# Moving two groups of buffers by 32 bytes within a partition: the split gated products of a mixture-of-experts kernel

## The chip, the cores and the metric

The kernel runs on one core of one Trainium2 chip. The metric is the device time of one execution in microseconds (us). The time before is the median of 3 runs, 1145.75 us (1145.21 to 1145.89).

## The reference, cut to what matters

The input is 16 sequences of 512 tokens with 128 features. Each goes through two residual steps:

```
x = x + layernorm(y),  y = C h + D * n,  h = causal convolution of B n,  n = layernorm(x)
x = x + layernorm(sum over 8 experts e of cw[e] * ( (silu(n G[e]) * (n U[e])) W[e] )),  n = layernorm(x)
```

The weights cw come from two softmaxes over the 8 experts. G, U and W are 128x512, 128x512 and 512x128 for each expert. This second step is nearly all of the work: for each of the 16 sequences ("blocks" b), each of the 8 experts e and each of the four quarters fc of the 512 hidden features, one tile of 128 hidden features x 512 tokens is computed and multiplied back down. That makes 16 x 8 x 4 = 512 tiles, numbered n.

## The kernel before, in words

**Splitting.** Products on TensorE use a 4-byte format (fp32r) that doesn't hold all of an fp32 number's digits. So each operand is split into two: a high part (`hi`, the number cast to fp32r) and a low part (`lo`, the number minus its high part). A product is then three matmuls, written in `mm3` (lines 336 to 339): weight-high by data-high (L337), weight-low by data-high (L338), weight-high by data-low (L339). The weight is the stationary operand of 128x128, which a separate instruction loads; the data are the moving operand of 128x512, which is streamed past it.

**One tile.** `up(n)` makes two such groups, g (gate) and uu (up), from the normalized and split input `xh`, `xl` of the block. ScalarE (ACT) takes the SiLU of g (L563). `gate` multiplies by uu on VectorE (DVE, L574); the result is called uu when it stays where it was, hh when it is put into SBUF. `split_hi` casts it on ACT into a buffer `hi` (L579), and `split_lo` subtracts on DVE or on GpSimd (POOL) into a buffer `lo` (L585). Four tiles later (LAG), `down(n)` streams that `hi` and `lo` past the third weight and accumulates the output d. Every four tiles `combine` multiplies d by the expert's weight and adds it up (L600, L605, L608). So TensorE's steady sequence is nine matmuls of 512 columns per tile: g three times, uu three times, d three times, with moving operands xh xh xl, xh xh xl, hi hi lo.

**Other work.** The front of the next blocks (layernorm, the convolution by a scan, the routing) and the back of the last ones are generators, cut into steps that the loop over n places by costs noted for DVE, ACT and POOL (`steps`, `take`, SLOT = 1.94 us). They add short groups to TensorE: bu (three matmuls of the same size, with moving operands `uh`, `ul`), yp and lg (small ones).

**Where buffers lie.** Memory on chip (SBUF) is addressed in bytes within each of 128 partitions. The pools are laid out in the order in which they are opened: const (weights, tables), fe (the blocks' inputs and intermediates: xh, xl, uh, ul and more), small (coefficients of a few bytes), and h, called `hp` in the code. hp holds `hi` and `lo` (5 buffers each of 2048 bytes), and sg, hh and ct (2 each). The total of the pools ahead decides at which byte hi and lo begin. In the built program every weight part and xh, xl, uh and ul begin 64 bytes past a multiple of 1024. All ten buffers hi and lo, and sg, hh and ct, begin 992 past one. The steps within a weight (the four quarters fc) are 512 bytes.

The first weights are loaded into buffers of hi and lo before these have other use, and two buffers of lo (`spare`) serve the first block.

Of the kernel before, what the change touches and what calls it, by code (L numbers as in the profile page):

```python
# [11 lines left out]
F32 = mybir.dt.float32  # L12
# [7 lines left out]
P = 128  # L20
# [27 lines left out]
def sandwich(ctx, tc, x, a_params, B_w, C_w, Dv, w_router, w_gating, w_gate, w_up, w_down, sines, out):  # L48
# [6 lines left out]
    small = pool("small", 3)  # L55
# [24 lines left out]
            nc.sync.dma_start(out=xts[b][:, k], in_=x[b].rearrange("(c p) d -> p c d", p=P)[:, k])  # L80


    spare = [hp.tile([P, F], F32R, name=f"spare{i}", tag="lo", bufs=LAG + 1).bitcast(F32) for i in range(2)]


# [785 lines left out]
```

## Time and profile before

| | |
|---|---|
| median of 3 runs | 1145.75 us |
| time of the profiled execution | 1146.53 us |
| its span, first to last instruction | 1144.7 us |
| granted TensorE clock, mean over the span | 0.997 |
| busy: PE, weight loads, DVE, ACT, POOL | 1121.9, 913.7, 870.9, 710.3, 764.9 us |
| HBM traffic | 61 GB/s |

PE is TensorE's matmuls and PEld its weight loads, which overlap them. A matmul's recorded length is not its share of the time: the next one starts while the last columns of the one before still pass through. The pace is the distance from one start to the next, and the timeline shows it.

### The profile page before, as it was taken

Reading aid. Unit: us, or ns where it says so; the run is one execution under the profiler, and the core shown is the slowest. Engines: PE = TensorE matmul, PEld = TensorE weight load, DVE = VectorE, ACT = ScalarE, POOL = GpSimd, SP = SyncE. Lnnn points to the kernel's source line nnn. Section 1 sums busy time; section 2 is a strip of 40 time slices with the busy share of each in tenths; the row PEclk is TensorE's granted clock in tenths of the full one; section 3 lists DMA queues with packets and bytes.
Section 4 is the critical chain, followed back from the end, with each engine's and each line's share of the span. In section 5 each row is a group of like instructions: output and inputs, shape, how many; then the busy total and the mean of one; then the engine's idle time right before and its main releaser. Section 6 shows DMA issues by size and latency. Waiting matters only on the chain.

```text
span 1144.7 us, 16089 instructions
## 1 busy us (share of the span) xinstructions
PE 1121.9 (98%) x4969; PEld 913.7 (80%) x4969; DVE 870.9 (76%) x2000; ACT 710.3 (62%) x1346; POOL 764.9 (67%) x641
## 2 busy tenths in 40 slices
PE   7999999999999999999999999999999999999997
PEld 4678787888888888888888888888888888888885
DVE  7878777787878778787777878777777877867666
ACT  3775655665666665666666665666666565666563
POOL 1788685775858668595866858677685776748452
PEclk9999999999999999999999999999999999999999
DMA  4140302203131120312202130121302202021120
GB/s 154 65 139 1 121 28 79 70 11 111 37 93 47 53 87 19 111 37 67 74 29 93 35 114 28 54 70 45 102 29 74 74 19 74 29 74 29 32 71 10
DMA packets 65894, 71.23 MB, mean 62 GB/s; under 512 B 8624, under 2 KB 50320, under 8 KB 65808
## 3 DMA queue, kind: packets, MB, share of 16 engines
q1 hardware_dynamic: 65392, 70.04, 19.8%
q8 instruction: 39, 0.64, 0.2%
q14 instruction: 47, 0.39, 0.1%
q10 hardware_dynamic: 416, 0.16, 0.1%
HBM read 54.98 MB, written 15.20 MB: 61 GB/s over the span
## 4 chain that ended last, share of the span: by engine, by line
PE 82%; DVE 2%; DMA 1%; issue 0%; ACT 0%; SPq 0%; DVEq 0%
PE d L337 9%; PE g L337 9%; PE d L338 9%; PE d L339 9%; PE g L338 9%; PE uu L337 9%; PE uu L339 9%; PE g L339 9%; PE uu L338 9%; PE yp L386 1%; PE lg L414 1%; DVE uu L574 1%; DMA cwb<-scw 0%; DVE lo L585 0%; ACT hi L579 0%
## 5 line engine op out<-in xcount | busy, mean ns | idle before, releaser
L579 ACT CAST hi<-uu 128x512 fp32r<-128x512 f32 x334 | 195.9, 587 | 219.7 <-DVE uu L574 200.4
L585 POOL TENSOR_TENSOR lo<-hh,hi 128x512 fp32r<-128x512 f32 x178 | 233.5, 1312 | 147.4 <-ACT hi L579 144.6
L563 ACT ACTIVATE sg<-g 128x512 f32<-128x512 f32 x512 | 306.7, 599 | 22.5 <-PE g L339 16.7
L585 DVE TENSOR_TENSOR lo<-uu,hi 128x512 fp32r<-128x512 f32 x334 | 229.1, 686 | 113.0 <-ACT hi L579 107.0
L574 DVE TENSOR_TENSOR uu<-sg,uu 128x512 f32<-128x512 f32 x334 | 231.2, 692 | 108.6 <-ACT sg L563 102.0
L608 POOL TENSOR_TENSOR acc<-acc,ct 128x512 f32<-128x512 f32 x109 | 145.3, 1333 | 119.2 <-DVE ct L605 107.1
L579 ACT CAST hi<-hh 128x512 fp32r<-128x512 f32 x178 | 110.6, 621 | 163.9 <-DVE hh L574 161.6
L337 PE MATMUL g<-xh,wgh 128*128 128x512 f32 x512 | 205.8, 402 | 2.3 <-ACT sg L563 1.5
L337 PE MATMUL uu<-xh,wuh 128*128 128x512 f32 x512 | 200.3, 391 | 5.7 <-DVE lo L585 5.7
L337 PE MATMUL d<-hi,wdh 128*128 128x512 f32 x512 | 203.5, 397 | 0.0
L338 PE MATMUL d<-hi,wdl 128*128 128x512 f32 x512 | 201.9, 394 | 0.0
L338 PE MATMUL g<-xh,wgl 128*128 128x512 f32 x512 | 201.3, 393 | 0.0
L339 PE MATMUL d<-lo,wdh 128*128 128x512 f32 x512 | 201.0, 393 | 0.0
L339 PE MATMUL g<-xl,wgh 128*128 128x512 f32 x512 | 199.8, 390 | 0.0
L339 PE MATMUL uu<-xl,wuh 128*128 128x512 f32 x512 | 199.6, 390 | 0.0
L338 PE MATMUL uu<-xh,wul 128*128 128x512 f32 x512 | 199.5, 390 | 0.0
L432 POOL TENSOR_TENSOR ez<-bases,ez 128x8 f32<-128x8 f32 x120 | 195.0, 1641 | 0.0
L574 DVE TENSOR_TENSOR hh<-sg,uu 128x512 f32<-128x512 f32 x178 | 120.9, 679 | 14.4 <-ACT sg L563 8.5
L337 PEld LDWEIGHTS uu<-xh,wuh 128*128 128x128 f32 x512 | 96.2, 188 | 29.9 <-DVE lo L585 7.9
L337 PEld LDWEIGHTS g<-xh,wgh 128*128 128x128 f32 x512 | 96.3, 188 | 25.8 <-ACT sg L563 4.6
L339 PEld LDWEIGHTS d<-lo,wdh 128*128 128x128 f32 x512 | 96.9, 189 | 23.4
L339 PEld LDWEIGHTS g<-xl,wgh 128*128 128x128 f32 x512 | 96.4, 188 | 23.2 <-DVE xl L754 0.4
(173 smaller groups left out, 1330.0 us busy)
## 6 DMA issues: line engine op xcount, KB each, us to landing
cwb<-scw SPq DMA_DIRECT2D x64, 512.0 KB
xt<-in_L_attn_u_dram SPq DMA_DIRECT2D x15, 256.0 KB
sco<-ob SPq DMA_DIRECT2D x60, 64.0 KB
ot<-sco SPq DMA_DIRECT2D x15, 256.0 KB
out_dram<-x SPq DMA_DIRECT2D x15, 256.0 KB
scr_u<-blk_u SPq DMA_DIRECT2D x52, 64.0 KB
ft_u<-scr_u SPq DMA_DIRECT2D x13, 256.0 KB
scr_x<-blk_x SPq DMA_DIRECT2D x52, 64.0 KB
```

The source lines that it names most:

```text
L337: pe.matmul(ps, w[0][:, cs], mh, start=first, stop=False)
L338: pe.matmul(ps, w[1][:, cs], mh, start=False, stop=False)
L339: pe.matmul(ps, w[0][:, cs], ml, start=False, stop=last)
L386: pe.matmul(yp[:, c], v[:, P * c : P * c + P], cT, start=True, stop=True)
L414: pe.matmul(lg[:, 2 * c : 2 * c + 2], xT[:, P * c : P * c + P], wrg.rearrange("d g e -> d (g e)"), start=True, stop=True,)
L432: gp.tensor_tensor(ez[:, i], bases.rearrange("p c g e -> p (c g) e")[:, i], ez[:, i], ALU.pow)
L563: act.activation(s, g, AF.Silu)
L574: vec.tensor_tensor(h, s, u, ALU.mult)
L579: act.copy(hi, pend[n])
L585: (gp if lo_pool[n] else vec).tensor_tensor(lo, h, hi.bitcast(F32), ALU.subtract)
L608: add = lambda: eng.tensor_tensor(acc, acc, t, ALU.add)
```

## The change

One tile of 8 fp32 numbers (32 bytes of each partition) is allocated in the pool small. Nothing writes or reads it.

```
@@ -80,6 +80,7 @@
             nc.sync.dma_start(out=xts[b][:, k], in_=x[b].rearrange("(c p) d -> p c d", p=P)[:, k])
 
 
+    small.tile([P, 8], F32, name="fill", bufs=1)
     spare = [hp.tile([P, F], F32R, name=f"spare{i}", tag="lo", bufs=LAG + 1).bitcast(F32) for i in range(2)]
```

In the built program the instructions of every engine are the same, in the same order, with the same operands and waits. The start addresses of the tiles of small and of hp are 32 bytes higher; those of const and fe, of PSUM and of DRAM stay. So hi, lo, sg, hh and ct begin at a multiple of 1024 bytes in place of 992 past one. Line numbers from 83 on rise by one.

More of the change, by code (lines that the diff above doesn't have):

```diff
@@ L80, in load_x @@
             nc.sync.dma_start(out=xts[b][:, k], in_=x[b].rearrange("(c p) d -> p c d", p=P)[:, k])
+    small.tile([P, 8], F32, name="fill", bufs=1)
     spare = [hp.tile([P, F], F32R, name=f"spare{i}", tag="lo", bufs=LAG + 1).bitcast(F32) for i in range(2)]
```

## The prediction

> **What bounds the kernel now.** First I read the page: busy shares and slices.
>
> ```profile
> PE 1121.9 (98%) x4969; PEld 913.7 (80%) x4969; DVE 870.9 (76%) x2000; ACT 710.3 (62%) x1346; POOL 764.9 (67%) x641
> ...
> PE   7999999999999999999999999999999999999997
> ```
>
> PE is busy 98% of the span. A high share alone could hide short waits, so next I asked for busy time by stretches, and for PE's waits in the long middle one.
>
> ```profile
> 75.00:200.00 125.00, 121.47 (x544) 98.82 (x543) 95.17 (x217) 77.70 (x150) 91.69 (x77) 1.00 0.20 65
> 200.00:1125.00 925.00, 925.00 (x4131) 760.79 (x4131) 704.54 (x1536) 581.50 (x1093) 630.41 (x515) 1.00 0.19 59
> ```
>
> The columns are the length, then busy time of PE, PEld, DVE, ACT, POOL, then clock and DMA. From 200 to 1125 us PE is busy 925.00 of 925.00, the clock is full, and the list of PE's waits in that stretch is empty. In these 925 us nothing but PE's own pace counts: matmuls times the distance from start to start.
>
> So third, that pace by kind: PE's groups in a clean stretch of 40 us.
>
> ```profile
> L339 PE MATMUL g<-xl,wgh 128*128 128x512 f32 x20 | 7.8, 389 | 0.0
> L337 PE MATMUL uu<-xh,wuh 128*128 128x512 f32 x20 | 7.8, 389 | 0.0
> ...
> L337 PE MATMUL d<-hi,wdh 128*128 128x512 f32 x19 | 7.6, 397 | 0.0
> L337 PE MATMUL g<-xh,wgh 128*128 128x512 f32 x19 | 7.5, 395 | 0.0
> L338 PE MATMUL d<-hi,wdl 128*128 128x512 f32 x19 | 7.5, 394 | 0.0
> L339 PE MATMUL d<-lo,wdh 128*128 128x512 f32 x19 | 7.4, 392 | 0.0
> ```
>
> The number before the last bar is the mean recorded length. Four of the nine kinds are at 389 ns (two uu rows are left out here); g's second, also left out, is at 393. The three d are at 397, 394, 392, and the two g that follow d at 395 and 393. Size, clock and weight loads (188 ns each) are the same. The nine lengths sum to 3527 ns; nine times 389 is 3501. The tile pays 26 ns over the fast kind.
>
> A recorded length is not a pace, so fourth the timeline, where no d stands among the matmuls and where nothing but d does.
>
> ```profile
> 274.54 0.39 PE L337 MATMUL g<-xh,wgh 128*128 128x512 f32 x1
> ...
> 275.90 0.40 PE L337 MATMUL d<-hi,wdh 128*128 128x512 f32 x1
> ...
> 1133.73 0.39 PE L337 MATMUL d<-hi,wdh 128*128 128x512 f32 x1
> ...
> 1136.31 0.40 PE L339 MATMUL d<-lo,wdh 128*128 128x512 f32 x1
> ```
>
> From 274.54 to 275.90 lie six matmuls of g and uu that follow a bu group and not d: 1.36 / 6 = 226.7 ns each. From 1133.73 to 1136.31 lie eleven of d alone at the end: 2.58 / 11 = 234.5 ns. And a whole tile in the steady part takes (271.78 - 230.45) / 20 = 2.0665 us between starts of the same kind. Six at 226.7 leave 706 ns for three d, 235.5 each. So a group that streams hi and lo costs 23 (by the tail) to 26 ns (by the tile) more than one that streams xh and xl. The two slow g after d are aftermath of d: where bu follows d, its first two are slow in the same way (273.85 to 274.31), and the g after bu are not.
>
> **Why the buffers may be the reason.** What differs between d and the other kinds? The weights of all begin 64 past a multiple of 1024, their quarters step by 512 bytes, and the four quarters have the same pace. The PSUM bank isn't it: behind d, bu writes yet another bank and shows the steps of g. The slot of hi and lo (five of each) doesn't show. What is left is where the moving operand begins: xh, xl, uh, ul at 64 past 1024, hi and lo at 992. The first is a multiple of 64, the second 32 off one. After the change hi and lo are multiples of 64 as well.
>
> **The change part by part.**
>
> *Instructions:* none added, removed or moved. No queue (SP's and POOL's included) holds anything new, and no wait is added.
>
> *Streaming hi and lo on PE.* No row shows a start at a multiple of 1024. The nearest are xh, xl and uh, ul, 226.7 ns. I take that: the gain per tile is 2066.5 - 9 x 226.7 = 26 ns. From 200 to 1125 us there are 432 tiles: 11.3 us. Before 200 us about 35 tiles run at the regular pace where PE carries the chain: 0.9 us. From 165 to 197 us the chain of waits runs along DVE (uu L574, lo L585, ct), and a DMA of 4.08 us (cwb<-scw); what PE saves there, 16 x 0.026 = 0.4 us, it waits away, and I count none. After 1125 us four tiles and the last d groups: 0.2 us. Sum 12.4 us.
>
> *The other engines' accesses to the moved tiles* (hi, lo, sg, hh, ct, and small). Compare the same operation on tiles that stay: ACT's cast of hh is 621 ns, of ft_x and ft_u 612 and 616; POOL's subtraction 1312 against 1292; DVE's product hh 679, the product v<-bu,tre 686. So between 9 ns less and 7 more each on ACT and DVE, and 20 less on POOL. This is worth nothing to the end: per tile DVE has 704.54 / 432 = 1.63 us of work, POOL 1.46, ACT 1.35, beside 2.07 for PE. That work covers it, also at 2.04. Were the cover gone, three operations of 7 ns on a tile would be 21 ns x 432 = 9 us, but it is far from gone.
>
> *Two rules of the Trainium skill speak against a gain of this size.* The page SBUF — State Buffer, Specifications, says SBUF is read in lines of 16 bytes and crossing lines is what costs. 992 and 1024 are both multiples of 16, so by that rule this change moves nothing and the time stays 1145.75. But in the rows streams of one size at one clock, all on whole lines of 16, differ by 8 to 9 ns, so the rule can't be all of it; I take the rows. The page TensorE: Matmul & The Clock Gate, Back-to-back issue gap, gives a full-clock matmul 512 / 2.4 + 2.5 = 216 ns. No kind here reaches it; the fastest is 226.7. By the rule there would be 3 x (235.5 - 216) = 58 ns in d alone, an estimate; that is my bound for the gain, 432 x 58 = 25 us.
>
> **The sum.** Profiled execution 1146.53 - 12.4 = 1134.1 us (span about 1132.3). The median of the runs is 0.78 us below the profiled one: 1133.3 us.
>
> **Rivals.**
>
> *The steady rhythm is lost (slower).* PE has two rhythms for the same aligned streams. After stops and after lg or yp it goes 224, 231, 236 ns, mean 230.4; then it falls into the even 226.7. At 42.37 to 44.46 us a tile takes 2.09 us, and again to 46.56, so the uneven rhythm can last. Later each such spell ends within one tile, and d stands in each of those tiles: it may be d's odd start that shifts PE into the even rhythm. If with hi and lo aligned nothing shifts it, nine matmuls cost 9 x 230.4 = 2073.6 ns, 7 more than now: 432 x 7 = +3.0 us, 1148.8. For it: lg and yp disturb PE some 30 times, and a spell could last until the next disturbance. Against: at 30.15 us, before any d, PE falls into 227 at once after a stop. The point: between 2040 and 2073.6, today's 2066.5 is passed when 79% of the tiles run unevenly.
>
> *The start isn't the reason (no change).* Then d is slow for something I don't see, and 1145.75 stays. For it: only one row, d, has the other start, so the case rests on exclusion. Against: bank, slot, quarter, size and weight start are excluded by rows.
>
> *A multiple of 1024 is not like 64 past it.* It is a third place, relative to weights at 64. If PE's two streams (weights and data) meet in memory, their distance counts: before 928 mod 1024, xh 0, after 960. Bound below: 216 ns per d matmul, -25 us, 1120. Bound above: once more what the odd start costs now, 432 x 26 ns = +11.3 us, 1157. Between these I keep to the nearest rows, at 226.7.
>
> **How the numbers follow.** Even pace for d as for xh, in full or most of it: 0.60, 1133.3. Better than that: 0.08, 1120 to 1130. No change: 0.08. Rhythm lost: 0.11, about 1148.8. A worse place: 0.13, up to 1157. Faster 0.68, same 0.08, slower 0.24; 0.2% (2.3 us) is about what a measurement of this kernel can tell from no change. The likeliest case's own range is 1130 to 1138 (gain of 8 to 16 us); both signs hold chance, so the range goes from 1128 to 1149, over no change and the lost rhythm. It leaves out most of the worse and better places, under 2 in 10.
>
> **What would show it.** Right: in the same clean stretch all nine PE kinds at 389 ns, a tile of 2.04 us, the d-only tail at 226.7 per step, and PE still without waits from 200 us on. Rhythm lost: steps of 224, 231, 236 in long runs, lengths of 387, 393, 397 in all kinds. No change: d still at 397, 394, 392. A worse place: d above 397, or weight loads above 188. If PE's list of waits after 200 us isn't empty, then another engine became late, and my cover was wrong.

## The result, and the profile after

The changed kernel is slower: 1152.25 us (median of 4, 1151.0 to 1152.59) against 1145.82 us for the kernel before (median of 4) in the same measurement; ratio 1.0051, 95% interval 1.0035 to 1.0067. The prediction was 1133.3 us, with a range from 1128 to 1149. Its profiled execution took 1152.28 us, with a span of 1150.5 us where before it was 1144.7.

First the page's busy shares and PE's row of slices (all line numbers are one higher than before), then the stretches.

```profile
PE 1127.7 (98%) x4969; PEld 912.8 (79%) x4969; DVE 874.9 (76%) x2000; ACT 712.8 (62%) x1346; POOL 764.4 (66%) x641
...
PE   6999999999999999999999999999999999999997
```

```profile
200.00:1125.00 925.00, 925.00 (x4108) 754.91 (x4108) 702.62 (x1531) 580.71 (x1087) 627.52 (x513) 1.00 0.19 59
```

PE is again busy 925.00 of 925.00 us, its list of waits in that stretch is again empty, and the mean clock reads 1.00. But it got through 4108 matmul records in place of 4131. So PE waits for nothing more; its own pace is slower. The clean stretch of 40 us, by kind:

```profile
L339 PE MATMUL g<-xh,wgl 128*128 128x512 f32 x20 | 7.9, 397 | 0.0
L338 PE MATMUL uu<-xh,wuh 128*128 128x512 f32 x20 | 7.9, 395 | 0.0
L340 PE MATMUL g<-xl,wgh 128*128 128x512 f32 x20 | 7.8, 389 | 0.0
L338 PE MATMUL d<-hi,wdh 128*128 128x512 f32 x19 | 7.5, 394 | 0.0
L339 PE MATMUL d<-hi,wdl 128*128 128x512 f32 x19 | 7.5, 394 | 0.0
L340 PE MATMUL d<-lo,wdh 128*128 128x512 f32 x19 | 7.5, 394 | 0.0
L339 PE MATMUL uu<-xh,wul 128*128 128x512 f32 x19 | 7.5, 393 | 0.0
L340 PE MATMUL uu<-xl,wuh 128*128 128x512 f32 x19 | 7.4, 389 | 0.0
L338 PE MATMUL g<-xh,wgh 128*128 128x512 f32 x19 | 7.4, 388 | 0.0
```

The three d, whose buffers moved, are level at 394, where they were 397, 394 and 392. The loss is in g and uu, whose buffers did not move: g's second went from 393 to 397, uu's first and second from 389 to 395 and 393, and only g's first got shorter, from 395 to 388. Before, two of these six were slow; now it is three. For the pace, the timeline: starts of g's first matmul, and of d at the end.

```profile
230.56 0.39 PE L338 MATMUL g<-xh,wgh 128*128 128x512 f32 x1
...
249.28 0.39 PE L338 MATMUL g<-xh,wgh 128*128 128x512 f32 x1
...
1138.76 0.39 PE L338 MATMUL d<-hi,wdh 128*128 128x512 f32 x1
...
1142.03 0.40 PE L340 MATMUL d<-lo,wdh 128*128 128x512 f32 x1
```

Nine tiles in 18.72 us are 2.080 us each, 13.3 ns more than 2.0667. At the end, where d stands alone, 14 steps take 3.27 us, 233.6 ns each: there d is a little faster than before (234.5). From the start of tile 80 to that of tile 511 the kernel takes 928.03 us, before 922.30. The 5.73 us between them are 431 x 13.3 ns, and nearly all of the 5.8 us between the spans. The clock has no part in these 5.73 us: ahead of them it was last lowered between 195 and 205 us in both kernels (from 200 to 205 us it reads 0.76 before and 0.84 after, from 205 to 210 us 1.00), and tile 80 starts at 209.4 us in both. The steps of a tile, from the timeline in nanoseconds: before 232, 231, 227, 227, 227, 227, 234, 232, 231 (g, uu, d); after 226, 236, 228, 233, 231, 227, 233, 233, 233.

### The profile page after: what moved, and what is told of

The parts are those of the page before. It is cut to its first block, busy times and chain, and to the rows that moved or that the text cites. A ratio compares the mean times of both kernels' runs of the same rounds, so it can differ in the third digit from the quotient of the medians.

```text
span 1150.5 us, 16089 instructions
## 1 busy us (share of the span) xinstructions
PE 1127.7 (98%) x4969; PEld 912.8 (79%) x4969; DVE 874.9 (76%) x2000; ACT 712.8 (62%) x1346; POOL 764.4 (66%) x641
## 4 chain that ended last, share of the span: by engine, by line
PE 91%; DVE 4%; issue 1%; ACT 1%; POOL 1%; DMA 1%; SPq 0%; DVEq 0%; POOLq 0%; ACTq 0%
PE d L340 10%; PE d L339 10%; PE uu L338 10%; PE g L339 10%; PE d L338 10%; PE g L338 10%; PE uu L339 10%; PE uu L340 10%; PE g L340 10%; PE yp L387 1%; PE lg L415 1%; DVE uu L575 1%; DVE lo L586 1%; ACT hi L580 0%; ACT sg L564 0%
## 5 line engine op out<-in xcount | busy, mean ns | idle before, releaser
L586 POOL TENSOR_TENSOR lo<-hh,hi 128x512 fp32r<-128x512 f32 x178 | 233.7, 1313 | 148.4 <-ACT hi L580 143.2
L338 PE MATMUL uu<-xh,wuh 128*128 128x512 f32 x512 | 202.9, 396 | 6.5 <-DVE lo L586 6.5
L338 PE MATMUL g<-xh,wgh 128*128 128x512 f32 x512 | 203.0, 396 | 1.6 <-ACT sg L564 1.1
L340 PEld LDWEIGHTS uu<-xl,wuh 128*128 128x128 f32 x512 | 96.5, 189 | 22.8
```

Source lines behind the costliest of these rows:

```text
L338: pe.matmul(ps, w[0][:, cs], mh, start=first, stop=False)
L340: pe.matmul(ps, w[0][:, cs], ml, start=False, stop=last)
L586: (gp if lo_pool[n] else vec).tensor_tensor(lo, h, hi.bitcast(F32), ALU.subtract)
```

## The experiments

Theory A was the prediction's: a stream's pace depends on where its data begin, and the place of xh is the fast one. Rivals: the other moved tiles (B), the lost rhythm (C). Later theories are named where they are put up.

### Four places, and the other tiles alone

```
-    small.tile([P, 8], F32, name="fill", bufs=1)
+    small.tile([P, 24], F32, name="fill", bufs=1)    # hi_at_64; 16: hi_at_32; 40: hi_at_128
```

> The fill is 96 bytes in place of 32: hi, lo, sg, hh and ct begin 64 past a multiple of 1024, the place of xh, xl and all weights. Theory A (a stream's pace depends on where its data begin, and 64 past 1024, or the place of the weights, is the fast one): all nine matmuls at 226.7 ns, a tile of 2.04 us, about 1133 us. Theory B (d is slow for something other than its place, and the 6 us of the change come from other tiles that moved): d stays at 392 to 397 ns recorded and the time lies at 1146 to 1152. Theory C (rhythm: with no odd start PE never falls into the even steps): 224, 231, 236 in long runs, 2.074 us a tile, 1149.

Measured: 1134.27 us (median of 4), ratio to before 0.9893, interval 0.987 to 0.9917. Its clean stretch, PE by kind:

```profile
L340 PE MATMUL uu<-xl,wuh 128*128 128x512 f32 x20 | 7.8, 389 | 0.0
L338 PE MATMUL d<-hi,wdh 128*128 128x512 f32 x20 | 7.8, 389 | 0.0
L339 PE MATMUL d<-hi,wdl 128*128 128x512 f32 x20 | 7.8, 389 | 0.0
L340 PE MATMUL d<-lo,wdh 128*128 128x512 f32 x20 | 7.8, 389 | 0.0
L338 PE MATMUL g<-xh,wgh 128*128 128x512 f32 x20 | 7.8, 389 | 0.0
```

All kinds are at 389 (four rows not shown too); a tile takes 2.040 us. So the start of hi and lo is what made d slow, and the price of an even tile was right. B and C fall. What was wrong is which place is the fast one. This version beats both kernels.

> The fill is 64 bytes: hi, lo, sg, hh and ct begin 32 past a multiple of 1024. If only the remainder by 64 counts, this is the kernel before over again: 2.067 us a tile, 1146 us. If the distance to the weights counts over more than 64 bytes (32 short of them, before 96 short, after the change 64 short), the steps differ from all three: no number, but a tile other than 2.067 and 2.080 us.

Measured: 2.067 us a tile, 1143.92 us (one run). The time is as the first reading has it, and the second reading's "a tile other than 2.067" missed. But the steps are not before's (d 234, 235, 232 and then 232, 227: one slow g in place of two), so it is a like sum and not the same case.

> The fill is 160 bytes: hi, lo, sg, hh and ct begin 128 past a multiple of 1024. If the remainder by 128 counts, this is the changed kernel over again (0 past): d at 233.3 ns a step, a tile of 2.080 us, 1152 us. If the remainder by 64 counts, it is like 64 past. If the distance to xh or to the weights counts by its size, 64 away on the other side may give another tile than 2.080.

Measured: 2.087 us a tile, 1153.81 us (one run). The d-only tail steps 229, 231, 226 (mean 228.7), and yet the tile is the slowest of all. 0 and 128 are not alike, and neither is like 64: neither a remainder by 64 nor one by 128 decides. And a stream that is nearly as fast as xh by itself can slow the others most.

```
+    hp.tile([P, 8], F32, name="fill", bufs=1)     # behind hi and lo, ahead of sg, hh, ct
     wrg = const.tile([D, 2, E], F32, name="wrg")
```

> The 32 bytes are put into the pool h behind hi and lo: hi and lo stay at 992, sg, hh and ct go to 0 as in the change; the tiles of small stay too. Theory A (PE's streams of hi and lo alone): the kernel before, 2.067 us a tile, 1146 us. Theory B (the other engines' accesses to the moved tiles slow PE): 2.080 us a tile, 1152 us.

Measured: 2.067 us a tile, with before's steps; 922.36 us from tile 80 to 511 (before 922.30). The time, 1149.86 us (one run), is longer by what happened ahead of tile 80: that one starts at 212.6 us in place of 209.4, with 6.8 us at half clock from 72.8 us on. The other engines' tiles have no part in PE's pace.

### Place, or distance from the weights

Theory P: the data's own place counts. Theory M: data of two places in turn cost by themselves. Theory W: what counts is the distance between data and weights, that is, the start of the data less the start of the weights.

```
-    wrg = const.tile([D, 2, E], F32, name="wrg")
+    wrg = small.tile([D, 2, E], F32, name="wrg", bufs=1)    # all weights, xh, xl 64 bytes lower
+    small.tile([P, 8], F32, name="fill", bufs=1)
```

> The router weights' small tile goes to the pool small, so that all weights and xh, xl, uh, ul begin 64 bytes lower, at a multiple of 1024; with the fill of the change hi and lo begin there as well. Theory W (the distance of the data from the weights counts): distance 0 for all, all nine at 226.7 ns, 2.040 us a tile, 1134 us. Theory M (what costs is data of two different places in turn): the same, 2.040. Theory P (a multiple of 1024 is a slow place in itself, 233.3 ns as the tail of the changed kernel shows): nine times 233.3, 2.100 us a tile, 1161 us.

Measured: 2.040 us a tile, 1134.23 us (one run; before beside it 1146.24). Everything is at the change's own place, a multiple of 1024, and fast. P falls.

```
+    const.tile([P, 16], F32, name="fill3")     # data_64_weights_0: behind the weights, besides wrg and the fill
...
+    fe.tile([P, 16], F32, name="fill2", bufs=1)     # data_128_weights_64: ahead of xh, with a fill of [P, 24]
```

> All weights begin at a multiple of 1024, 64 bytes lower than before; xh, xl, uh, ul, hi and lo all begin 64 past one, as in the run with hi at 64. Theory P (the data's own place counts) and theory M (one place for all data): 2.040 us a tile, 1134 us. Theory W: all data are 64 past the weights, which gave 229, 231, 226 ns (mean 228.7) in the d-only tail of the run with hi at 128; nine times 228.7 is 2.058 us a tile, about 1142 us.

> 64 bytes of fill ahead of xh and 96 ahead of hi: all data begin 128 past a multiple of 1024, the weights stay at 64. Theory W (distance 64): 228.7 ns a step, 2.058 us a tile, 1142 us, the same as with data at 64 and weights at 0. Theory M: 2.040 us, 1134 us. Theory P: 128 gave 2.087 us beside xh at 64; alone its tail gave 228.7, so 2.058. W and P part in the run with weights at 0.

Measured: 2.060 us a tile in both, 1142.94 and 1143.53 us (one run each). The data of all nine matmuls lie at one place, so M alone gives 2.040 and falls as the only cause; W's 2.058 is met within 2 ns by two kernels whose data and weights lie at different places, but in both 64 bytes apart. The first g of a tile, eight tiles apart, with all at 0 and then with the data at 64 and the weights at 0:

```profile
230.37 0.39 PE L338 MATMUL g<-xh,wgh 128*128 128x512 f32 x1
...
246.69 0.39 PE L338 MATMUL g<-xh,wgh 128*128 128x512 f32 x1
...
229.33 0.39 PE L338 MATMUL g<-xh,wgh 128*128 128x512 f32 x1
...
245.81 0.40 PE L338 MATMUL g<-xh,wgh 128*128 128x512 f32 x1
```

16.32 / 8 = 2.040 us, and 16.48 / 8 = 2.060.

> The fill is 608 bytes: hi and lo begin 576 past a multiple of 1024, 512 from the place of xh, xl and the weights. If places repeat every 512 bytes (the four quarters of a weight, 512 bytes apart, show the same pace), this is the run with hi at 64 again: 226.7 ns a step, 2.040 us a tile, 1134 us. If they repeat only every 1024, the d rows are slow, 2.06 us or more.

Measured (fill of [P, 152]): 2.040 us a tile, 1134.97 us (one run). It repeats after 512 bytes at the latest.

### TensorE alone

The next kernel drops everything but the streams: mm3 on one data tile read from a chosen byte, with six weight tiles.

```
+    for k in range(32):
+        last = bank("solo_" + LETTERS[k])
+        for n in range(12):
+            mm3(last, W[2], n % 4, at(k))
...
+            mm3(g, W[0], n % 4, at(0))
+            mm3(u, W[1], n % 4, at(0))
+            mm3(d, W[2], n % 4, at(k))
```

> TensorE alone: the kernel's matmuls of 512 columns with their weight loads, and nothing beside them on any engine; all the rest of the computation is left out, and the output is not the reference's. All weights and the data tile begin at one remainder by 512; the data are read from k x 16 bytes on, k from 0 to 31. First 36 matmuls per k with that start for all (solo_a to solo_F), then for each even k 12 tiles of nine: six at distance 0 and three at k x 16 bytes (mixg, mixu, mixd). Theory W (the distance between data and weights sets PE's pace, PE needs no other engine for it): solo 226.7 ns at distance 0, about 228.7 at 64, 233.3 at 448 (the change's place, 64 short), 234.5 at 416 (before's place); and the mix repeats the kernels: 2.067 us a tile at 416, 2.080 at 448, 2.067 at 480, 2.087 at 64, 2.040 at 0. If the other engines' accesses have a part in it, the mix shows other numbers than the kernels, 2.04 to 2.05 for all. Which distance is best is open.

The timeline's first g of a tile, eight tiles apart, at a distance of 416 bytes (A: before's, 96 short of the next 512), 448 (C: the change's, 64 short) and 0 (a):

```profile
288.81 0.39 PE L80 MATMUL mixg_a<-data,wgh 128*128 128x512 f32 x1
...
305.13 0.39 PE L80 MATMUL mixg_a<-data,wgh 128*128 128x512 f32 x1
...
612.28 0.40 PE L80 MATMUL mixg_A<-data,wgh 128*128 128x512 f32 x1
...
628.81 0.40 PE L80 MATMUL mixg_A<-data,wgh 128*128 128x512 f32 x1
...
637.11 0.39 PE L80 MATMUL mixg_C<-data,wgh 128*128 128x512 f32 x1
...
653.75 0.39 PE L80 MATMUL mixg_C<-data,wgh 128*128 128x512 f32 x1
```

16.32 / 8 = 2.040, 16.53 / 8 = 2.066, 16.64 / 8 = 2.080 us. With DVE and POOL idle, TensorE repeats both kernels, even step by step: at 448 it goes 226, 236, 228, 233, 231, 226, 234, 233, 233. So no other engine is needed for the effect, and all of W's numbers are met. The table has steps of the streams alone (mean of 30 steps; those at k and k + 256 bytes agree within 1 ns) and the tile of nine.

| distance, remainder by 256 bytes | step alone, ns | tile of nine, us | in the full kernel, us a tile |
|---|---|---|---|
| 0 | 226.7 | 2.040 | 2.040 (hi at 64, hi at 576, all at 0) |
| 32 | 233.3 | 2.087 | |
| 64 | 228.9 | 2.087 | 2.087 (hi at 128) |
| 96 | 233.5 | 2.073 | |
| 128 | 232.3 | 2.080 | |
| 160 | 234.2 | 2.067 | 2.067 (before) |
| 192 | 233.3 | 2.080 | 2.080 (the change) |
| 224 | 233.3 | 2.067 | 2.067 (hi at 32) |
| 240 | 226.7 | not run | |

Distances repeat by 256 bytes, and the change moved d from 160 to 192. No distance in steps of 16 bytes beats 226.7; the slowest is 208, with 234.7.

> The fill is 352 bytes: hi and lo begin 256 past the place of xh, xl and the weights. The run with TensorE alone showed 226.7 to 227 ns at a distance of 256 as at 0. If that holds in the whole kernel: 2.040 us a tile, 1134 us. If only whole 512 repeat here: d slow, 2.06 us or more.

Measured in the full kernel (fill of [P, 88]): 2.040 us a tile, 1136.3 us (one run). The 256 hold.

> TensorE alone again; everything else of the computation is left out and the output is not the reference's. Part 1: the weight load is cut from 128 columns to 64 and 32 (width_l, width_m, width_s), with the data 0, 160 and 192 bytes from the weights (_a, _b, _c). Theory X (the load that runs beside a stream takes memory turns from it): the step shrinks with the load, at 32 columns to 219 ns or less at all three distances, and the differences between distances shrink as well. Theory Y (the start of a stream costs by its distance, whatever is loaded): 226.7, 234.2 and 233.3 stay. Part 2: the data stay, and the weights begin k x 32 bytes later (shift_a to shift_p). If only the distance counts, shift by s gives what data at 256 - s gave: 226.7 at 0 and 256, 234 at 96, 233 to 234 at most others. Part 3: weights and data of d both 160 (botha) or 192 bytes (bothb) from those of g and uu. Theory M (data of two places in turn cost by themselves): 2.067 and 2.080 us a tile as in the first run. Theory W: d runs at distance 0 and only the two streams at its borders meet other loads, under 2.060.

Part 1, recorded lengths of matmuls and, in the last line, of a load (l: loads of 128 columns, s: of 32; a: distance 0, b: 160):

```profile
L81 PE MATMUL width_l_b<-data,wdh 128*128 128x512 f32 x12 | 4.8, 396 | 0.0
...
L81 PE MATMUL width_s_b<-data,wdh 128*32 128x512 f32 x12 | 4.7, 395 | 0.0
...
L81 PE MATMUL width_s_a<-data,wdh 128*32 128x512 f32 x12 | 4.7, 394 | 0.0
...
L81 PE MATMUL width_l_a<-data,wdh 128*128 128x512 f32 x12 | 4.7, 389 | 0.0
...
L81 PEld LDWEIGHTS width_s_a<-data,wdh 128*32 128x32 f32 x12 | 1.3, 109 | 1.4
```

The load fell from 188 to 109 ns, and the steps became 231.8, 230.9 and 231.6 ns at distances 0, 160 and 192: the differences shrink to 1 ns, which fits a load that meets the stream, but the step doesn't fall to 219. With 64 columns (134 ns) it is in between: 230.0, 231.5 and 232.7. At distance 0 the pace is slower with a shorter load. X is right about the distances and wrong about the rest; Y falls. With fewer weight columns a matmul also writes fewer rows of the result (32 in place of 128), so the load isn't shown to be the only cause. Part 2: moving the weights by 32, 96, 192 and 256 bytes gives 233.4, 234.3, 228.8 and 226.7 ns, which is the table at 224, 160, 64 and 0; all 16 shifts agree with it within 0.5 ns. So it is the distance, with its sign, and not the place of either. Part 3: 2.071 and 2.089 us in turn at 160, 2.065 and 2.081 at 192, W's "under 2.060" missed; the means, 2.080 and 2.073, miss M's 2.067 and 2.080 as well.

```
+    wd = pool("wd", 1)     # weights of d at a multiple of 512, with fills ahead and behind
-        W[j, e] = [const.tile([P, F], F32R, name=f"w{'gud'[j]}{i}{e}") for i in "hl"]
+        W[j, e] = [(wd if j == 2 else const).tile([P, F], F32R, name=f"w{'gud'[j]}{i}{e}") for i in "hl"]
```

> hi and lo keep the place that the change gives them (a multiple of 512), and the weights of d, in a pool of their own, are put at a multiple of 512 as well; weights of g and uu, and xh, xl, stay 64 past one. Theory W (distance of the data from the weights loaded beside them): d at distance 0, so that the change's place costs less than before: under 2.060 us a tile and under 1143 us. Theory P or M (the place of hi and lo in itself, or data of two places in turn): 2.080 us and 1152 us stay.

Measured: 2.073 us a tile in the mean, 1147.97 us (one run; before beside it 1146.3). From tile 80 to tile 511 it takes 925.31 us, between before's 922.30 and the change's 928.03. The expectation under 2.060 missed as in part 3 at 192, with the same number, and so did the 2.080 of P and M. Every stream here has distance 0 from its own weights, so the distance that counts is not, or not only, that one. Two things are left. The weights that are loaded beside the last uu and the last d, for the group that comes next, lie at distances of 64 and 192 from these streams, as they do in part 3 at 192; and the data change their place twice in a tile. The first is the likelier cause, since the two runs with all data 64 bytes from all weights are slow without any change of place. But that a change of the data's place costs something besides (theory M as a second cause) isn't excluded: no run here parts the two.

### Own step and aftermath

```
+                for n in range(groups):     # 1, 3 or 9 groups of three
+                    mm3(d, W[2], n % 4, at(4 * k))
+                for n in range(12):
+                    mm3(g, W[n % 2], n % 4, at(0))
```

> TensorE alone, the rest of the computation left out, so the output is not the reference's. 3, 9 or 27 matmuls with their data 160, 192 or 64 bytes from the weights (odd_a, odd_b, odd_c), each followed by 36 at distance 0 (after_), six times over. Theory R (two terms: a stream's own step at its distance, and an aftermath, the matmuls at distance 0 that pass before the even 226.7 is back): over 226.7 ns each, the block with n odd ones costs n x 7.5 + a at 160, n x 6.6 + a at 192, n x 2.2 + a at 64, with the same a for each n. From the tiles of nine: a about 4 at 160 (before), 20 at 192 (the change) and 40 at 64 (hi at 128), and the steps after at 192 need six matmuls where at 160 they need three. Theory S (no fixed aftermath: where no odd stream follows at once, the uneven rhythm lasts on through all 36, or the excess depends on n in no such order): excess beyond 60 ns with three odd ones, and uneven steps to the end of the 36.

Starts of blocks of 3 + 36 matmuls, four blocks apart, at 160 (ax), 192 (bx) and 64 (cx):

```profile
23.85 0.40 PE L80 MATMUL odd_ax<-data,wdh 128*128 128x512 f32 x1
...
59.31 0.40 PE L80 MATMUL odd_ax<-data,wdh 128*128 128x512 f32 x1
...
225.82 0.39 PE L80 MATMUL odd_bx<-data,wdh 128*128 128x512 f32 x1
...
261.34 0.39 PE L80 MATMUL odd_bx<-data,wdh 128*128 128x512 f32 x1
...
427.69 0.40 PE L80 MATMUL odd_cx<-data,wdh 128*128 128x512 f32 x1
...
463.35 0.40 PE L80 MATMUL odd_cx<-data,wdh 128*128 128x512 f32 x1
```

A block takes 8.865, 8.880 and 8.915 us by these lines, and 8.867, 8.880 and 8.913 to the nanosecond. Less 39 x 226.67 ns (2.040 us / 9), the excess is 27, 40 and 73 ns with three odd matmuls; with nine it is 67, 80 and 87; with 27 it is 247, 200 and 127. At 192 this is a line: 20 + 6.67 for each odd one. At 64 it is 67 + 2.2 each. At 160 it is no line (6.7 each from three to nine, 10 each from there on). After three odd ones, the steps are 233, 230 and then even at 160; 226, 236, 228, 233, 230 and then even at 192; ten uneven at 64. At 192 and 64 that stays so after nine and 27; at 160 one uneven step follows nine and ten follow 27. Theory R holds at 192 and 64. Of S, the first half falls, since all return to 226.7; at 160 the excess follows no line, as its second half has it. R's a at 64 was guessed too low, 40 for 67: ten uneven steps don't fit between two d of a tile, which are six matmuls apart.

## Why the prediction was wrong, point by point

**What bounds the kernel:** right. PE has no wait from 200 to 1125 us before and after, and nearly the whole difference is its pace. Two small slips change nothing in it: the clock was not full from the start of that stretch (0.76 from 200 to 205 us), and 706 / 3 is 235.3, not 235.5.

**The start of hi and lo makes d slow:** right for these weights, and now shown by moving it. An even tile of 2.040 us and about 1133 us were the price of d at xh's place; hi at 64 has 2.040 and 1134.27.

**"The nearest are xh, xl and uh, ul, 226.7 ns. I take that":** this step failed. It took a multiple of 1024 to be like 64 past one, as both are multiples of 64. No row showed that; xh differs from hi in its remainder, but in its distance from the weights too, and the latter counts. The change moved d from a distance of 160 to 192 by 256, one slow distance to another, so the booked gain of 26 ns a tile was a loss of 13.3. The third rival named that distance and had it at 13% on the slow side with 1157 as its bound; the range stopped at 1149 and so left it out. Its signs did not come either (d above 397, or loads above 188): d is at 394, the loads at 188, and the loss is in g and uu.

**The aftermath as a part of d's cost:** the two slow g behind d were booked as 10 of the 26 ns that would go with d. It is a term of its own. In the trial with TensorE alone, the steps of three odd matmuls at 160 are 17 ns over the even pace together and those after them 10; at 192 it is 20 and 20. So 27 ns became 40, +13 as in the kernel, and 10 of the 13 are in matmuls whose buffers did not move. d alone in a long row is faster at 192 (233.3 ns) than at 160 (234.2), but in threes it gains nothing. Where the one term ends and the other begins is uncertain by about a step, as a step is counted from start to start.

**The lost rhythm:** its side was right, its mechanism was not. The tile of 2.080 us is longer than the 2.0736 that it gave for a rhythm lost throughout. PE does fall back into the even steps, after five uneven ones in place of two, and when all data are at distance 0 (hi at 64) it stays there.

**Other engines:** right. ACT's cast is 587 and 621 ns, POOL's subtraction 1313, DVE's subtraction 686, all within 1 ns of before, and moving sg, hh and ct alone left the tile at 2.067.

**The two rules of the Trainium skill:** lines of 16 bytes (SBUF — State Buffer, Specifications) gave no change; moves by multiples of 32 bytes made between 11 us less and 8 us more, and the trial in steps of 16 went from 226.7 to 231.6 in one. To set that rule aside was right. The 216 ns of TensorE: Matmul & The Clock Gate, Back-to-back issue gap, which the section gives as the gap of an isolated matmul, were met at none of 32 distances, so the lower bound of 1120 was out of reach.

**Open:** why 256 bytes and this sign, whether a change of the data's place costs something by itself, what holds the even pace at 226.7, and why a load of 32 columns brings 231 at distance 0. That the loads and the streams meet in memory fits the runs; none shows the place where they meet.

## What to carry to other kernels

Where one engine never waits, compare the pace of its like instructions by kind: 8 ns between streams of the same size was worth 11 us here. Before booking a gain from moving a buffer, ask what else differs between the slow and the fast row besides the property that the change sets; here two properties went together. The safe change gives the slow buffer exactly the fast one's place, here a fill of 96 bytes in place of 32. For streams like these (fp32r, 512 columns, a weight load for each matmul), keep data and weights that meet on TensorE at the same remainder by 256 bytes, and judge a place by the whole sequence, not by the moved stream alone.

## What the runs showed of the hardware that was not expected

TensorE's pace with a weight load for each matmul of 512 columns goes from 226.7 (distances 0 and 240) to 234.7 ns (208) with the distance between data and weights by 256 bytes, without any other engine at work. A stream at another distance leaves an aftermath in the matmuls that follow: in the trial between 3 ns (nine at 160) and 50 (three at 64), by the steps. A distance of 64, among the faster by itself (228.9 ns), has the longest aftermath of the three that were tried (160, 192, 64), and with 32 it makes the slowest tile (2.087 us). A shorter weight load (109 for 188 ns) did not make an even stream faster, but slower, 231.8 for 226.7.
